# First layer of a convolution-attention network: the softmax denominators of two query blocks formed together on the rows of the taps

## The chip, the cores and the metric

The kernel runs on one core of a Trainium2 chip. The metric is device time in microseconds (us) of one execution; the median of three runs before the change is 6046.56 us (6038.23 to 6056.44). The core has a matrix engine (PE, with its weight loads PEld), a vector engine (DVE), a scalar engine (ACT), a general engine (POOL) and a queue for DMAs (SP), each with its own instruction stream in order. Matmul results land in PSUM, in eight banks of 128 partitions x 512 float32 each. All data here are float32.

## The reference, cut to what matters

Two images of 512 channels x 64 x 64 positions pass through four layers. The first layer, the only one that the change touches, is an attention with 8 heads of 64 channels. Each query looks at 9 local keys (a 3x3 window, the "taps") and at 256 pooled keys, with one softmax over both:

```python
attn_local = jnp.einsum('bhnd,bhndk->bhnk', q_scaled, k_local)
attn_pool = jnp.einsum('bhnd,bhpd->bhnp', q_scaled, _l2norm(k_pool))
attn = jax.nn.softmax(jnp.concatenate([attn_local, attn_pool], axis=-1), axis=-1)
a_local, a_pool = (attn[..., :ll], attn[..., ll:])
lt = jnp.einsum('bhnd,hdk->bhnk', q_norm, learnable_tokens) + learnable_bias[None] + a_local
x_local = jnp.einsum('bhnk,bhndk->bhnd', lt, v_local)
x_pool = jnp.einsum('bhnp,bhpd->bhnd', a_pool, v_pool)
```

So each query and head has one denominator, the sum of 9 + 256 exponentials, and its reciprocal is needed twice: on the 9 local weights, before a learned term is added, and on the 64 channels of the pooled part.

## The kernel before, in words

Class Local computes the first layer. A unit is 128 channels (two heads) and 1024 queries (two blocks j = 0, 1 of 512), so there are 16 units per image, and a loop in run() goes through them as a pipeline. One pass of the loop for unit u projects k, q and v of later units (projections, norms, value; L133 is the matmul of project), forms the tap products of unit u + 1 (tap_products, L1972, and tap_sums, L1985 and L2000), attends for unit u (attend) and weighs for unit u - 1 (weigh). The stages are generators that are advanced one step each per round, ten or so rounds per pass; this gives the order in which instructions are written down. It is a priority, not the final order: the program's builder moves an instruction ahead of an earlier one on the same engine when it finds the earlier one not ready, and then fixes the order.

What the prediction's steps touch:

- PSUM: five banks named mm are shared by all of these matmuls; one bank (tap) holds the tap sums and two (qs) a copy of the queries. A matmul that finds no free mm bank waits until ACT or DVE has read one out.
- attend, block by block: scores (L2017) and exponentials (L2021) for two halves of the 256 pooled keys; values (L2027), copied out by ACT (L2029); POOL adds the exponentials of the two halves (L2031). Then the denominators: two matmuls with ones over these sums (L2036) and two over el, the exponentials of the taps (L2040), give psD, in which the 64 rows of each head hold its denominator. DVE takes the reciprocal in two halves (L2049) and POOL multiplies the attended values by it (L2051). Block 0 does this in rounds 4 and 5, block 1 in rounds 7 and 8.
- el has four groups of 32 rows, two per block; of a group 18 rows are in use, 9 taps of head 0 and then 9 of head 1, and the even and odd taps lie in different groups. It is ready one pass before attend needs it.
- weigh, rounds 1 to 9 of the next pass: four matmuls (L2085) pick the reciprocals of the two heads and put them on the tap rows in PSUM; DVE multiplies el by them (L2087) and adds the learned part (L2088). Then for each tap and block a matmul spreads the weight to the channels (L2096), DVE multiplies it with the shifted values (L2102) and POOL adds the product to the attended values (L2107). Taps 6 and 7 fall in round 8, tap 8 in round 9. The result goes to DRAM.
- norms in round 1: four matmuls spread the norms of the new k and q (L1897), and DVE multiplies them in (L1905), which frees four mm banks. In round 8 POOL takes a power (L1932) for the next norms.
- output, in the last three passes and after: the output projection (L1808), with POOL additions of the bias (L1813) and DVE work (L1814, L1815).

Of the kernel before, what the change touches and what calls it, by code (L numbers as in the profile page):

```python
# [11 lines left out]
ALU = mybir.AluOpType  # L12
# [3 lines left out]
P = 128  # L16
C = 512
# [3 lines left out]
TB = 512  # L21
# [10 lines left out]
(C_ID, C_GRP, C_MEAN, C_ONE, C_E2, C_TAP, C_Y, C_X, C_MH, C_ROW, C_TAPW, C_E32, C_SR,  # L32
    C_SD) = (0, 128, 256, 384, 512, 514, 540, 572, 573, 589, 717, 757, 789, 821)
C_N = 949
# [1512 lines left out]
class Local:  # L1547
# [9 lines left out]
    def __init__(self, net, X, Y, sp_scale, d, wp, yp, pp, ppt, pps):  # L1557
# [18 lines left out]
        late = new([P, 12 * TB + 3 * TB], "late")  # L1576
# [4 lines left out]
        self.recips = part.ring([P, TB], 2)  # L1581
# [3 lines left out]
        self.gelus = Lent(late[:, 12 * TB:]).ring([P, TB], 3)  # L1585
# [391 lines left out]
    def tap_sums(self, u):  # L1977
# [4 lines left out]
        def sums(k):  # L1982
            for j in range(2):
                q = 2 * j + k % 2
                nc.tensor.matmul(ps[32 * q:32 * q + 32, :],  # L1985
                                 self.cst[:, C_TAPW + 8 - k:C_TAPW + 40 - k],
                                 self.prods[k % 3][:, j * TB:(j + 1) * TB], start=(k < 2),
                                 stop=(k > 6))
# [15 lines left out]
    def attend(self, u):  # L2004
# [5 lines left out]
        prob, R = {}, []  # L2010
        self.out[u] = out, R
# [11 lines left out]
        def values(j):  # L2023
# [5 lines left out]
            nc.scalar.copy(out[:, j * TB:(j + 1) * TB], psO)  # L2029
            for h in range(2):  # L2030
                nc.gpsimd.tensor_tensor(prob[j, 1][h], prob[j, 0][h], prob[j, 1][h], ALU.add)  # L2031

        def sums(j):
            psD = self.bank()
            for h, c in enumerate(heads):
                nc.tensor.matmul(psD[c, :], self.net.one[:, :HD], prob[j, 1][h], start=True,  # L2036
                                 stop=False)
            b = slice(j * HD, (j + 1) * HD)
            for h, c in enumerate(heads):
                nc.tensor.matmul(psD[c, :], self.cst[b, C_SD + h * HD:C_SD + (h + 1) * HD],  # L2040
                                 el[b, :], start=False, stop=True)
            return psD

        def ends(j, psD):
            r = self.recips()

            for i in range(2):
                part = slice(i * TB // 2, (i + 1) * TB // 2)
                nc.vector.reciprocal(r[:, part], psD[:, part])  # L2049
            o = out[:, j * TB:(j + 1) * TB]  # L2050
            nc.gpsimd.tensor_tensor(o, o, r, ALU.mult)  # L2051
            R.append(r)
# [9 lines left out]
        n = sums(0)  # L2062
        exponentials(1, 1)
        yield
        ends(0, n)
# [3 lines left out]
        n = sums(1)  # L2069
        yield  # L2070
        ends(1, n)
        yield

    def weigh(self, u):
# [3 lines left out]
        out, R = self.out.pop(u)  # L2078
        el, lt = self.el.pop(u), self.lt.pop(u)
        yield  # L2080
        ps = self.bank()
        for j in range(2):
            for g in range(2):
                q = 2 * j + g
                nc.tensor.matmul(ps[32 * q:32 * q + 32, :], self.cst[:, C_SR:C_SR + 32], R[j],  # L2085
                                 start=True, stop=True)
        nc.vector.tensor_tensor(el, el, ps, ALU.mult)  # L2087
        nc.vector.tensor_tensor(el, el, lt, ALU.add)  # L2088
        yield
# [75 lines left out]
def arrays_of(i):  # L2165
# [19 lines left out]
    cst[:HD, C_TAPW + 8] = 1  # L2185
# [3 lines left out]
    row = p % 32  # L2189
    cst[0, C_SR:C_SR + 9] = 1  # L2190
    cst[HD, C_SR + 9:C_SR + 18] = 1
    for h in range(2):
        mine = (row // 9 == h) & (row % 9 % 2 == p // 32 % 2)
        cst[:, C_SD + h * HD:C_SD + (h + 1) * HD] = mine[:, None]
# [22 lines left out]
    for q in range(4):  # L2217
        vec[32 * q:32 * q + 18, V_LBR:V_LBR + 4] = vec[:18, V_LB:V_LB + 4]
# [5 lines left out]
    tapb[:, :18] = taps  # L2224
# [7 lines left out]
        "taps": taps, "tapb": tapb.reshape(P, 9, P), "tok32": np.pad(tok, ((0, 0), (0, 0), (0, 14))),  # L2232
# [31 lines left out]
```

## Time and profile before

| what | value |
|---|---|
| median of 3 runs | 6046.56 us (6038.23 to 6056.44) |
| profiled execution | 6069.55 us, its span 6067.8 us |
| mean granted PE clock | 0.954 |
| PE busy in the span | 5607.9 us (92%) |
| DVE, ACT, POOL busy | 3101.9, 1466.3, 1604.9 us |
| first layer's units, first image, 300 to 1250 us | PE 913.24, DVE 540.37, POOL 589.59 us |
| first layer's units, second image, 3370 to 4290 us | PE 884.45, DVE 536.80, POOL 579.77 us |

In the group lines below, a line names the source line, the engine, the operation, the tiles written and read with their shapes, the count; then total busy time and mean ns of one; then the engine's idle time just before and what ended it. A matmul in float32 has two records. In the timeline lines, the columns are start and duration in us, engine, line, operation, tiles, and in brackets the idle time before and its releaser. A window line gives the window, its length, the busy time and count of PE, PEld, DVE, ACT and POOL, the granted PE clock, and the DMAs' share and GB/s.

### The profile page before, as it was taken

To read this page: it belongs to the slowest core of one execution; us is meant where nothing else is said; L and a number is where in the kernel's file an instruction comes from. 1 tells how busy PE (TensorE), PEld (TensorE's weight loads), DVE (VectorE), ACT (ScalarE), POOL (GpSimd) and SP (SyncE) were. 2 spreads that over 40 slices of the span, in tenths; PEclk is the share of its full clock that TensorE was granted. 3 is DMA by queue.
4 is the path that set the end of the run, shared out by engine and by line. 5 is a ranking of instruction groups with operands and counts; after the bars stand their busy time and mean duration, and the time that the engine had idled before them with its cause. 6 is when DMAs were issued, how large, how long until landed. Compare 5 with 4: busy or idle time off the path is not lost. (4 is left out here: it accounts for less than half of the span.)

```text
span 6067.8 us, 54683 instructions
## 1 busy us (share of the span) xinstructions
PE 5607.9 (92%) x21859; PEld 2361.9 (39%) x21859; DVE 3101.9 (51%) x3462; ACT 1466.3 (24%) x2633; POOL 1604.9 (26%) x1218
## 2 busy tenths in 40 slices
PE   7899999999978899999988999999999788999999
PEld 3333332455323344444343333324553334444443
DVE  3245556644669533444432555566456794334444
ACT  1232222114212222212112332220242132221221
POOL 0146657710320011100001566676003100110000
PEclk9899998999989999999988999999999899999999
DMA  3000000100000000100010000001000000000000
GB/s 131 2 6 16 13 12 30 47 35 9 1 0 0 29 1 1 56 14 35 28 51 2 6 16 16 11 28 52 30 9 0 0 0 16 1 8 9 20 14 22
DMA packets 50812, 118.32 MB, mean 20 GB/s; under 512 B 4018, under 2 KB 17074, under 8 KB 48756
## 3 DMA queue, kind: packets, MB, share of 16 engines
q1 hardware_dynamic: 50548, 114.73, 5.3%
q8 instruction: 175, 2.87, 0.2%
q14 instruction: 89, 0.73, 0.0%
HBM read 74.87 MB, written 39.85 MB: 19 GB/s over the span
## 5 line engine op out<-in xcount | busy, mean ns | idle before, releaser
L133 PE MATMUL mm<-big,w 128*128 128x512 f32 x2560 | 1219.1, 622 | 0.0
L2107 POOL TENSOR_TENSOR late<-late,big 128x512 f32<-128x512 f32 x576 | 717.3, 1277 | 523.3 <-DVE big L2102 511.5
L133 PEld LDWEIGHTS mm<-big,w 128*128 128x128 f32 x2560 | 479.4, 197 | 720.5 <-issue 623.9
L2102 DVE TENSOR_TENSOR big<-big,mm 128x512 f32<-128x512 f32 x576 | 363.2, 679 | 602.5 <-PE mm L2096 548.2
L1097 PE MATMUL acc<-big,dg 128*128 128x512 f32 x896 | 407.4, 614 | 79.8 <-DVE big L692 51.1
L692 DVE TENSOR_TENSOR big<-big 128x3968 f32<-128x3968 f32 x96 | 410.8, 4289 | 38.4 <-PE acc L1097 32.6
L1166 POOL TENSOR_TENSOR total<-prob 128x512 f32<-128x512 f32 x128 | 159.7, 1269 | 769.8 <-ACT prob L1163 769.8
L1430 DVE TENSOR_REDUCE tops<-mm 128x2 f32<-128x512 f32 x256 | 159.4, 681 | 290.8 <-PE mm L1271 290.8
L1242 POOL TENSOR_TENSOR sq<-q 128x512 f32<-128x512 f32 x64 | 66.6, 1041 | 905.6 <-ACT q L1240 905.6
L1097 PEld LDWEIGHTS acc<-big,dg 128*128 128x128 f32 x896 | 173.8, 197 | 312.0 <-issue 283.0
L1478 DVE RECIPROCAL recip<-psD 128x512 f32<-128x512 f32 x64 | 214.9, 3358 | 151.6 <-PE psD L1474 151.6
L2096 PE MATMUL mm<-late,tapb 18*128 18x512 f32 x1152 | 240.7, 665 | 54.0 <-DVE big L2102 28.3
L1183 DVE RECIPROCAL recip<-psD 128x512 f32<-128x512 f32 x64 | 214.9, 3358 | 87.1 <-PE psD L1180 87.1
L1330 ACT ACTIVATE big<-mm 128x512 f32<-128x512 f32 x256 | 153.1, 598 | 382.3 <-DVE top L1327 381.9
L1972 DVE TENSOR_TENSOR prod<-qs,big 128x1024 f32<-128x1024 f32 x192 | 228.9, 1207 | 29.3 <-PE tap L1985 29.3
L2049 DVE RECIPROCAL late<-mm 128x256 f32<-128x256 f32 x128 | 218.9, 1735 | 33.5 <-PE mm L2040 33.5
L133 PE MATMUL mm<-big,big 128*128 128x512 f32 x512 | 234.0, 619 | 0.0
L1309 PE MATMUL mm<-w,big 128*128 128x512 f32 x512 | 231.3, 601 | 0.0
L1932 POOL TENSOR_TENSOR wide<-norms,mhalf 128x32 f32<-128x32 f32 x34 | 185.1, 5443 | 168.6 <-DVE norms L1929 168.6
L133 PE MATMUL mm<-big,wq 128*128 128x512 f32 x512 | 228.7, 597 | 0.0
L547 PE MATMUL mm<-big,wo 128*128 128x512 f32 x512 | 224.5, 596 | 0.0
L547 PE MATMUL mm<-q,w 128*128 128x512 f32 x512 | 224.2, 596 | 0.0
(343 smaller groups left out, 7910.4 us busy)
## 6 DMA issues: line engine op xcount, KB each, us to landing
big<-in_x SPq DMA_DIRECT2D x8, 2048.0 KB, 10.6
yd<-late SPq DMA_DIRECT2D x32, 512.0 KB, 2.6
out<-big SPq DMA_DIRECT2D x16, 1024.0 KB, 4.2
big<-in_W_kv SPq DMA_DIRECT2D x8, 1024.0 KB, 11.1
big<-yd SPq DMA_DIRECT2D x16, 512.0 KB, 3.7
wd<-big SPq DMA_DIRECT2D x6, 1024.0 KB, 4.8
w<-wd SPq DMA_DIRECT2D x24, 256.0 KB, 3.0
prod<-yd SPq DMA_DIRECT2D x8, 512.0 KB, 4.3
```

The source lines that it names most:

```text
L133: self.nc.tensor.matmul(ps, w[:, kc, :], X[:, kc, blk * TB:(blk + 1) * TB], start=(kc == 0), stop=(kc == KC - 1))
L547: nc.tensor.matmul(ps, w[:, kc, oc * P:(oc + 1) * P], att[:, kc, :], start=(kc == 0), stop=(kc == KC - 1))
L692: nc.vector.tensor_tensor(o, a, b, ALU.max)
L1097: nc.tensor.matmul(accs[b], dg, src[:, b * TB:(b + 1) * TB], start=(j == 0), stop=(j == 6))
L1183: nc.vector.reciprocal(r, psD)
L1309: nc.tensor.matmul(ps, X[:, kc, lo:lo + P], wv[:, kc, :], start=(kc == 0), stop=(kc == KC - 1))
L1478: nc.vector.reciprocal(r, psD)
L1972: self.nc.vector.tensor_tensor(self.prods[k % 3].rearrange("p (y x) -> p y x", x=W), qs, self.kx[:, y + dy:y + dy + self.UY, dx:dx + W], A ...
L2049: nc.vector.reciprocal(r[:, part], psD[:, part])
L2096: nc.tensor.matmul(ps, self.tapb[32 * q:32 * q + 18, kk, :], el[32 * q:32 * q + 18, :], start=True, stop=True)
L2102: nc.vector.tensor_tensor(dst[:, j * TB:(j + 1) * TB].rearrange("p (y x) -> p y x", x=W), self.vx[:, y:y + self.UY // 2, dx:dx + W], ps.re ...
L2107: nc.gpsimd.tensor_tensor(o, o, dst[:, j * TB:(j + 1) * TB], ALU.add)
```

## The change

The tap rows of el are ordered tap by tap with the heads alternating (row 2 x tap + head) instead of head by head, and the constants follow. The sums of both blocks now go into one bank, once per unit: block j takes the 64 rows from 64 x j, and within them even rows hold head 0's denominator, odd rows head 1's (constants C_EVEN and C_SD). These rows line up with el's. So there is one reciprocal of 128 x 512 per unit (still in two halves), kept in a buffer of its own, and DVE multiplies el by it directly, from SBUF. For the channels, weigh spreads rows 64 x j and 64 x j + 1 of the reciprocal by one matmul per block with C_ROW, and DVE multiplies the attended values by the two banks; POOL's two multiplications are gone. The sums of the exponentials of block 0 go to buffers of their own (halves), since they are read later. The denominators are formed in rounds 7 and 8 for both blocks.

```diff
@@ -29,9 +29,9 @@
 RISKS = 16
 
 
-(C_ID, C_GRP, C_MEAN, C_ONE, C_E2, C_TAP, C_Y, C_X, C_MH, C_ROW, C_TAPW, C_E32, C_SR,
-    C_SD) = (0, 128, 256, 384, 512, 514, 540, 572, 573, 589, 717, 757, 789, 821)
-C_N = 949
+(C_ID, C_GRP, C_MEAN, C_ONE, C_E2, C_TAP, C_Y, C_X, C_MH, C_ROW, C_TAPW, C_E32, C_EVEN,
+    C_SD) = (0, 128, 256, 384, 512, 514, 540, 572, 573, 589, 717, 765, 797, 863)
+C_N = 927
 
 V_BQ, V_BK, V_BSR, V_LNG, V_LNB, V_QE, V_TEMP = 0, 4, 12, 16, 20, 24, 28
 V_WOFF, V_BOFF, V_BOUT, V_B2, V_B1, V_LB, V_WOFF2 = 32, 33, 34, 38, 42, 43, 47
@@ -1573,16 +1573,18 @@
         self.weighed = [weighed[:, i * self.UT:(i + 1) * self.UT] for i in range(2)]
         self.prods = [whole.take([P, self.UT])] + [new([P, self.UT], f"prod{i}") for i in range(2)]
         self.tok = whole.take([P, KC, 32])
-        late = new([P, 12 * TB + 3 * TB], "late")
+        late = new([P, 13 * TB + 3 * TB], "late")
         part = Lent(late)
         self.prob = part.ring([P, TB], 4)
         self.att = part.ring([P, self.UT], 2)
         self.els = part.ring([P, TB], 2)
-        self.recips = part.ring([P, TB], 2)
+
+        self.halves = [part.take([P, TB]) for _ in range(2)]
+        self.recip = part.take([P, TB])
         self.lts = part.ring([P, TB], 3)
 
         self.first = Lent(late[:, :12 * TB])
-        self.gelus = Lent(late[:, 12 * TB:]).ring([P, TB], 3)
+        self.gelus = Lent(late[:, 13 * TB:]).ring([P, TB], 3)
         self.raw_w = [w.rearrange("p (kc o) -> p kc o", kc=KC)
                       for w in (weighed, flat[:, 6144:8192])]
         self.w_sr = qs[:, :KC * C].rearrange("p (kc o) -> p kc o", kc=KC)
@@ -1983,7 +1985,7 @@
             for j in range(2):
                 q = 2 * j + k % 2
                 nc.tensor.matmul(ps[32 * q:32 * q + 32, :],
-                                 self.cst[:, C_TAPW + 8 - k:C_TAPW + 40 - k],
+                                 self.cst[:, C_TAPW + 16 - 2 * k:C_TAPW + 48 - 2 * k],
                                  self.prods[k % 3][:, j * TB:(j + 1) * TB], start=(k < 2),
                                  stop=(k > 6))
 
@@ -2007,8 +2009,8 @@
         cc = u // self.UN
         qs, el = self.qs[u % 3], self.el[u]
         out = self.att()
-        prob, R = {}, []
-        self.out[u] = out, R
+        prob = {}
+        self.out[u] = out
         heads = [slice(h * HD, (h + 1) * HD) for h in range(2)]
 
         def exponentials(j, k2):
@@ -2027,65 +2029,60 @@
                     nc.tensor.matmul(psO[c, :], self.vp[:, k2, cc * P + h * HD:][:, :HD],
                                      prob[j, k2][h], start=(k2 == 0), stop=(k2 == 1))
             nc.scalar.copy(out[:, j * TB:(j + 1) * TB], psO)
+            dst = prob[1, 1] if j else self.halves
             for h in range(2):
-                nc.gpsimd.tensor_tensor(prob[j, 1][h], prob[j, 0][h], prob[j, 1][h], ALU.add)
-
-        def sums(j):
+                nc.gpsimd.tensor_tensor(dst[h], prob[j, 0][h], prob[j, 1][h], ALU.add)
+
+        def sums():
             psD = self.bank()
-            for h, c in enumerate(heads):
-                nc.tensor.matmul(psD[c, :], self.net.one[:, :HD], prob[j, 1][h], start=True,
-                                 stop=False)
-            b = slice(j * HD, (j + 1) * HD)
-            for h, c in enumerate(heads):
-                nc.tensor.matmul(psD[c, :], self.cst[b, C_SD + h * HD:C_SD + (h + 1) * HD],
-                                 el[b, :], start=False, stop=True)
+            blocks = [slice(j * HD, (j + 1) * HD) for j in range(2)]
+            for h in range(2):
+                for j, b in enumerate(blocks):
+                    nc.tensor.matmul(psD[b, :], self.cst[:, C_EVEN + h:C_EVEN + h + HD],
+                                     (prob[1, 1] if j else self.halves)[h], start=(h == 0),
+                                     stop=False)
+            for b in blocks:
+                nc.tensor.matmul(psD[b, :], self.cst[b, C_SD:C_SD + HD], el[b, :], start=False,
+                                 stop=True)
             return psD
 
-        def ends(j, psD):
-            r = self.recips()
-
-            for i in range(2):
-                part = slice(i * TB // 2, (i + 1) * TB // 2)
-                nc.vector.reciprocal(r[:, part], psD[:, part])
+        exponentials(0, 0)
+        yield
+        exponentials(0, 1)
+        yield
+        values(0)
+        yield
+        exponentials(1, 0)
+        yield
+        exponentials(1, 1)
+        yield
+        values(1)
+        yield
+        yield
+        psD = sums()
+        yield
+
+        for i in range(2):
+            part = slice(i * TB // 2, (i + 1) * TB // 2)
+            nc.vector.reciprocal(self.recip[:, part], psD[:, part])
+        yield
+
+    def weigh(self, u):
+
+        nc = self.nc
+        cc, y0 = u // self.UN, u % self.UN * self.UY
+        out, R = self.out.pop(u), self.recip
+        el, lt = self.el.pop(u), self.lt.pop(u)
+        yield
+        banks = [self.bank() for _ in range(2)]
+        for j, ps in enumerate(banks):
+            q = slice(64 * j, 64 * j + 2)
+            nc.tensor.matmul(ps, self.cst[q, C_ROW:C_ROW + P], R[q, :], start=True, stop=True)
+        nc.vector.tensor_tensor(el, el, R, ALU.mult)
+        nc.vector.tensor_tensor(el, el, lt, ALU.add)
+        for j, ps in enumerate(banks):
             o = out[:, j * TB:(j + 1) * TB]
-            nc.gpsimd.tensor_tensor(o, o, r, ALU.mult)
-            R.append(r)
-
-        exponentials(0, 0)
-        yield
-        exponentials(0, 1)
-        yield
-        values(0)
-        yield
-        exponentials(1, 0)
-        yield
-        n = sums(0)
-        exponentials(1, 1)
-        yield
-        ends(0, n)
-        values(1)
-        yield
-        yield
-        n = sums(1)
-        yield
-        ends(1, n)
-        yield
-
-    def weigh(self, u):
-
-        nc = self.nc
-        cc, y0 = u // self.UN, u % self.UN * self.UY
-        out, R = self.out.pop(u)
-        el, lt = self.el.pop(u), self.lt.pop(u)
-        yield
-        ps = self.bank()
-        for j in range(2):
-            for g in range(2):
-                q = 2 * j + g
-                nc.tensor.matmul(ps[32 * q:32 * q + 32, :], self.cst[:, C_SR:C_SR + 32], R[j],
-                                 start=True, stop=True)
-        nc.vector.tensor_tensor(el, el, ps, ALU.mult)
-        nc.vector.tensor_tensor(el, el, lt, ALU.add)
+            nc.vector.tensor_tensor(o, o, ps, ALU.mult)
         yield
         for k in range(0, 9, 2):
             banks = {}
@@ -2182,16 +2179,14 @@
 
     cst[:, C_ROW:C_ROW + P] = p[:, None] % 32 == p[None, :] // HD
 
-    cst[:HD, C_TAPW + 8] = 1
+    cst[:HD, C_TAPW + 16] = 1
     cst[HD:, C_TAPW + 17] = 1
     cst[:, C_E32:C_E32 + 2] = p[:, None] // HD == np.arange(2)
 
-    row = p % 32
-    cst[0, C_SR:C_SR + 9] = 1
-    cst[HD, C_SR + 9:C_SR + 18] = 1
-    for h in range(2):
-        mine = (row // 9 == h) & (row % 9 % 2 == p // 32 % 2)
-        cst[:, C_SD + h * HD:C_SD + (h + 1) * HD] = mine[:, None]
+    row, half = p % 32, np.arange(HD)
+    cst[:, C_EVEN:C_EVEN + 66] = np.arange(66) % 2 == 0
+    mine = (row < 18) & (row // 2 % 2 == p // 32 % 2)
+    cst[:, C_SD:C_SD + HD] = mine[:, None] & (row[:, None] % 2 == half % 2)
     g = np.stack(np.meshgrid(np.arange(16), np.arange(16), indexing="ij")).reshape(1, 2, NK)
     a = {k: np.asarray(v) for k, v in i.items()}
 
@@ -2215,13 +2210,14 @@
     vec[:18, V_LB:V_LB + 4] = a["L0_conv_learnable_bias"].reshape(KC, 18).T
     vec[:, V_LBR:V_LBR + 4] = 0
     for q in range(4):
-        vec[32 * q:32 * q + 18, V_LBR:V_LBR + 4] = vec[:18, V_LB:V_LB + 4]
+        for h in range(2):
+            vec[32 * q + h:32 * q + 18:2, V_LBR:V_LBR + 4] = vec[9 * h:9 * h + 9, V_LB:V_LB + 4]
     vec[:, V_WOFF2:V_WOFF2 + 2] = np.tile(a["L1_conv_w_off2"].T, (2, 1))
 
     taps = (np.arange(18)[:, None, None]
             == 9 * (p[None, None, :] // HD) + np.arange(9)[None, :, None]).astype(f)
     tapb = np.zeros((4, 32, 9, P), f)
-    tapb[:, :18] = taps
+    tapb[:, :18] = taps.reshape(2, 9, 9, P).transpose(1, 0, 2, 3).reshape(18, 9, P)
     tok = np.zeros((P, KC, 18), f)
     t = a["L0_conv_learnable_tokens"].reshape(KC, 2, HD, 9).transpose(1, 2, 0, 3)
     tok[:HD, :, :9] = t[0]
@@ -2229,9 +2225,12 @@
     arrays = {
         "x": a["x"], "cst": cst, "grid": np.broadcast_to(g, (P, 2, NK)).astype(f),
         "vec": vec, "tok": tok,
-        "taps": taps, "tapb": tapb.reshape(P, 9, P), "tok32": np.pad(tok, ((0, 0), (0, 0), (0, 14))),
-
-        "row2": (p[:, None] % 32 == 2 + p[None, :] // HD).astype(f), "bv_row": b_kv[None, C:], "pb_rows": np.broadcast_to(a["L0_conv_b_proj"], (P, C)),
+        "taps": taps, "tapb": tapb.reshape(P, 9, P),
+        "tok32": np.pad(tok.reshape(P, KC, 2, 9).transpose(0, 1, 3, 2).reshape(P, KC, 18),
+                        ((0, 0), (0, 0), (0, 14))),
+
+        "row2": (p[:, None] % 32 == 2 + p[None, :] // HD).astype(f), "bv_row": b_kv[None, C:],
+        "pb_rows": np.broadcast_to(a["L0_conv_b_proj"], (P, C)),
         "bproj_row": a["L0_conv_b_proj"][None, :],
         "W_q": a["L0_conv_W_q"], "W_kv": a["L0_conv_W_kv"], "W_sr": a["L0_conv_W_sr"],
         "W_proj": a["L0_conv_W_proj"],
```

## The prediction

> **What bounds the kernel now.** I read the page first (span 6067.8 us, run 6069.55 us, median of the runs 6046.56 us), then windows by stage, the groups of the lines that the diff touches, one period engine by engine, and the waits.
>
> Busy time by window, second image, two periods (us; PE, PEld, DVE, ACT, POOL):
>
> ```profile
> 3799.30:3854.00 54.70, 53.36 (x210) 16.92 (x212) 31.88 (x40) 16.61 (x27) 35.20 (x26) 1.00 0.04 15
> 3854.00:3908.70 54.70, 53.36 (x210) 16.91 (x212) 31.88 (x40) 16.62 (x27) 35.20 (x26) 1.00 0.03 10
> ```
>
> A unit costs 54.70 us and PE is busy for 53.36 of them. There are 16 units per image and two images, so 1 us per unit is 32 us. PE works in order, so a late bank or operand stops all behind it. DVE (31.9) and POOL (35.2) have slack on average, not everywhere.
>
> Groups that the diff touches (busy, mean ns):
>
> ```profile
> L2049 DVE RECIPROCAL late<-mm 128x256 f32<-128x256 f32 x128 | 218.9, 1735 | 33.5 <-PE mm L2040 33.5
> L2051 POOL TENSOR_TENSOR late<-late 128x512 f32<-128x512 f32 x64 | 81.9, 1279 | 52.9 <-DVE late L2049 28.6 <-issue 15.1 <-ACT late L2021 6.5
> L2087 DVE TENSOR_TENSOR late<-late,mm 128x512 f32<-128x512 f32 x32 | 21.7, 677 | 0.4 <-PE mm L2085 0.4
> L2088 DVE TENSOR_TENSOR late<-late 128x512 f32<-128x512 f32 x32 | 56.3, 1758 | 1.0
> ```
>
> L2087 and L2088 have one shape, yet L2088 averages 1758 ns: its median is 692, its longest 9371. The timeline of DVE shows where:
>
> ```profile
> 3997.56 0.68 DVE L2087 TENSOR_TENSOR late<-late,mm 128x512 f32<-128x512 f32 x1
> 3998.27 9.37 DVE L2088 TENSOR_TENSOR late<-late 128x512 f32<-128x512 f32 x1
> ```
>
> and that of POOL over the same time:
>
> ```profile
> 3994.79 2.51 POOL L2107 TENSOR_TENSOR late<-late,big 128x512 f32<-128x512 f32 x2
> 3997.26 9.84 POOL L1813 TENSOR_TENSOR big<-big,kp 128x512 f32<-128x512 f32 x8
> ```
>
> L2088 adds two SBUF operands. It could not finish until eight back-to-back POOL additions were through; it did not slip in between two of them. L2087, L2102 and L1972 have one operand in PSUM and keep 0.68 and 1.2 us beside a busy POOL.
>
> The stretch where this matters, DVE in one period:
>
> ```profile
> 3822.75 1.75 DVE L2049 RECIPROCAL late<-mm 128x256 f32<-128x256 f32 x1
> 3825.84 0.69 DVE L2102 TENSOR_TENSOR big<-big,mm 128x512 f32<-128x512 f32 x1 [1.34 <-POOL late L2107]
> 3827.06 0.69 DVE L2102 TENSOR_TENSOR big<-big,mm 128x512 f32<-128x512 f32 x1 [0.54 <-POOL late L2107]
> 3827.67 1.22 DVE L1972 TENSOR_TENSOR big<-qs,big 128x1024 f32<-128x1024 f32 x1
> 3828.80 2.35 DVE L1972 TENSOR_TENSOR prod<-qs,big 128x1024 f32<-128x1024 f32 x2
> 3831.07 1.27 DVE L1905 TENSOR_TENSOR big<-big,mm 128x512 f32<-128x512 f32 x2
> 3833.45 0.68 DVE L2087 TENSOR_TENSOR late<-late,mm 128x512 f32<-128x512 f32 x1
> ```
>
> and POOL:
>
> ```profile
> 3824.52 4.98 POOL L2107 TENSOR_TENSOR late<-late,big 128x512 f32<-128x512 f32 x4
> 3829.43 1.30 POOL L2051 TENSOR_TENSOR late<-late 128x512 f32<-128x512 f32 x1
> 3830.65 2.55 POOL L2107 TENSOR_TENSOR late<-late,big 128x512 f32<-128x512 f32 x2
> ```
>
> POOL is busy without a gap from 3824.52 to 3833.20, and L2087 starts just after. And PE hangs on L1905 there (weight loads):
>
> ```profile
> 3831.80 0.29 PEld L2017 LDWEIGHTS mm<-big,kp 64*128 64x128 f32 x2 [0.92 <-DVE big L1905]
> 3833.45 0.30 PEld L133 LDWEIGHTS mm<-big,w 128*128 128x128 f32 x2 [0.76 <-DVE qn L1905]
> ```
>
> L1905 frees the banks for the next scores and the value projection: DVE has no slack here.
>
> [...] all PSUM readers in the page are DVE or ACT. [...] four 128x32 matmuls of L2085 took 1.0 us in all, as much as two 128x64 of L2036.
>
> **The change part by part**, per unit, from starts in this period.
> 1. First block's sums, gone: L2036 and L2040, 1.01 us each: -2.02 on PE. A 0.38 us bank wait before L2036 passes to the next scores.
> 2. The joint sums: four 128x64 (L2027 has this shape: 1.87 a call) and a pair of 64x64 (1.01) make 2.88 instead of 2.02. They end at 3816.01 + 2.88 = 3818.9, where the reciprocal began at 3818.76, and PE waits there anyway (L1985 at 3819.10, next matmul at 3821.11, of which 1.0 is work). So +0.2 of the +0.86 is on the path; without that wait all is.
> 3. Two reciprocal halves fewer, -3.37 on DVE, at 3853.98: worth 0, since DVE idles 7.71 us soon after. The other two halves stay.
> 4. L2051 twice, -2.56 on POOL: nothing waits for the first; the second shortens POOL's run to 3831.9.
> 5. The spread: two 2x128 matmuls for four 128x32: two row groups of L2096 took 1.06 us against 1.0, so 0. But it takes two of five banks, freed only after L1905 and the two new products on DVE: the second must await an L1905 that the scores awaited before. One L1905 step, 0.6; I take +0.5.
> 6. The two products of the attended values on DVE: no row has exactly this; L2102 has one SBUF and one PSUM operand, 0.68 each. They fall into the 4.45 us that DVE idles after 3834.86: 0; with that cover gone, 1.36.
> 7. el times R: as L2087, but R now lies in SBUF. Alone it costs 0.69, as L2088. Its place is the question.
>
> **Where el times R goes.** The order on an engine isn't that of the source: a second reciprocal half runs after four L2102, and two L1972 of later priority run ahead of L1905, which was not ready. L2087 ran late because it needed PE's spread. The new product needs only R and el, both done by 3824.5. By priority it comes after the L1972 of round 0 and ahead of the next two and, until PE delivers, of L1905. So it reaches DVE's head at 3828.8, in POOL's run. It waits to 3831.9 and ends at 3832.6; one L1972 (1.13) follows, and perhaps el+lt (0.62) and another L1972 (1.13), and L1905 starts at 3833.7 to 3835.5 instead of 3831.07: 2.7 to 4.4 late, I take 3.5. PE is late by as much.
> Sum: -2.02 + 0.2 + 0.5 + 3.5 = +2.2 per unit (1.4 to 3.1). Eleven weighing periods per image have both POOL's run behind them and L1905: 22 x 2.2 = +48 (31 to 68).
> Twice per image L1813 follows the run at once, so the product waits for both: to 4007.1 - 1.3 = 4005.8. L1905 then starts near 4008.5 and PE's L2096 near 4016, against 4007.79: about 8 late, less 1.8: +6.3, four times +25 (22 to 29). The first and the last two weighings per image meet an almost quiet POOL: 6 x -1.3 = -8.
> Total +65 (45 to 89): 6069.6 to 6135 for the profiled run, 6046.6 to **6112** for the median, 6070 to 6160 with the spread of the runs (18 us). The granted clock (0.94 to 1.00 by window) may give some back when PE idles.
>
> **Rivals.**
> - *Faster*: el times R runs behind L1905, at 3833.45 as L2087 did, after POOL's run. Then a unit gains 2.02 - 0.2 - 0.5 = 1.3: 32 x 1.3 = -42, 6005 (5990 to 6028). For it: DVE is in order and L2087 stands there now. Against: only its need of PE put it there. It decides if L1905 is delayed by under 1.3 us.
> - *Even*: the product is early but L1905 runs right after it, and PE has other work ready, so the delay is near 1.3: 6047, within 18. Against: the earliest end is already 3832.6.
> - *Slower still*: the product comes right after the reciprocal, at 3824.5, ahead of both L2102. It waits for POOL to run dry at 3829.5; both L2102 (1.3) and one to three more follow. L1905 is 3.8 to 5 late: 22 x 3.1 + 25 - 8 = +85, 6132 (6115 to 6150). Against: L2102 has the earlier round and now runs first.
>
> **How the numbers follow.** Forecast 0.57, slower still 0.13, faster 0.18, even 0.12. A measurement can tell 0.3% (18 us). Slower gets 0.57 + 0.13, and a little of the even case; same about 0.11; faster 0.18. The forecast's own range is 6070 to 6160. Leaving out most of the faster case (0.12) and the top (0.06), the range is 6012 to 6160.
>
> **What would show it.** Right: a two-SBUF DVE product at its new line averaging 2 to 5 us instead of 0.69, ended with a POOL L2107 group; PE weight loads waiting on L1905 for 3 us and more per period; periods of 56 to 58 us at full clock. Part 1 right: L1985 of round 4 about 2 us earlier after the second score pair. Wrong: if that product runs in 0.69 us each time, the periods should be near 53.4 us and the total near 6005. Also wrong if POOL lets DVE in between two additions, or if PE fills the wait with other matmuls.

## The result and the profile after

The changed kernel takes 6080.28 us (median of 4 runs, 6074.2 to 6085.03) against 6042.4 us (4 runs, 6036.85 to 6056.44): a ratio of 1.0059, 95% interval 1.0038 to 1.0080. It is slower by 38 us, where 65 were forecast. The span of its profiled execution is 6081.4 us against 6067.8 before, 13.6 us more. The two differences disagree since the profiled execution of the kernel before was itself 27 us over its median.

A period in a window of the changed kernel, second image, in the columns of the windows before (granted PE clock third from the end), and then stretches of that period, cut at PE's wait:

```profile
3835.80:3893.80 58.00, 55.33 (x204) 17.93 (x206) 30.46 (x38) 16.69 (x28) 33.66 (x24) 0.94 0.02 9
3845.80:3847.80 2.00, 2.00 (x12) 0.89 (x10) 2.00 (x2) 1.08 (x2) 2.00 (x2) 1.00 0.00 0
3847.80:3850.30 2.50, 0.50 (x3) 0.00 (x0) 2.50 (x5) 0.00 (x0) 1.88 (x2) 0.76 0.00 0
3850.30:3852.30 2.00, 1.96 (x2) 0.49 (x2) 2.00 (x4) 0.19 (x1) 0.00 (x0) 0.50 0.65 262
3852.30:3854.30 2.00, 2.00 (x5) 0.50 (x4) 0.97 (x2) 1.05 (x1) 0.00 (x0) 0.50 0.00 0
3854.30:3858.70 4.40, 4.40 (x10) 1.79 (x8) 0.00 (x0) 1.09 (x2) 2.48 (x2) 0.81 0.00 0
```

A period has gone from 54.70 to 58.00 us. DVE and POOL have less to do (31.88 to 30.46, 35.20 to 33.66). PE had 2.02 us taken off and 0.86 put on, so its busy time should have fallen by 1.16; it rose, from 53.36 to 55.33. The cut shows why: within the 2.5 us in which PE works for 0.50, its clock goes to half. By the clock records it is at half from 3849.11 to 3855.93, so it falls while PE still waits. So of the 3.3 us, -1.16 is the work, +1.33 is idle time (2.67 against 1.34), and some +3.1 is the same work at a lower clock. (Part of this stretching falls where PE would have waited; an experiment below puts the clock's net part at 2.5.)

The groups that the diff touches:

```profile
L2067 DVE RECIPROCAL late<-mm 128x256 f32<-128x256 f32 x64 | 111.4, 1749 | 21.3 <-PE mm L2045 21.3
L2081 DVE TENSOR_TENSOR late<-late 128x512 f32<-128x512 f32 x32 | 43.8, 1368 | 0.0
L2082 DVE TENSOR_TENSOR late<-late 128x512 f32<-128x512 f32 x32 | 27.6, 861 | 0.1
L2085 DVE TENSOR_TENSOR late<-late,mm 128x512 f32<-128x512 f32 x64 | 40.9, 674 | 0.0
```

L2081 is el times R, L2082 adds the learned part; the latter averaged 1758 ns before. Line numbers have moved: L1905 is now L1907, L1972 is L1974, L1985 is L1987, L2017 is L2019, L2107 is L2104. DVE in one period of the changed kernel, from its timeline:

```profile
3843.84 0.69 DVE L2099 TENSOR_TENSOR big<-big,mm 128x512 f32<-128x512 f32 x1 [0.54 <-POOL late L2104]
3844.44 1.22 DVE L1974 TENSOR_TENSOR big<-qs,big 128x1024 f32<-128x1024 f32 x1
3845.57 1.25 DVE L2081 TENSOR_TENSOR late<-late 128x512 f32<-128x512 f32 x1
3846.74 1.21 DVE L1974 TENSOR_TENSOR prod<-qs,big 128x1024 f32<-128x1024 f32 x1
3847.88 0.67 DVE L2082 TENSOR_TENSOR late<-late 128x512 f32<-128x512 f32 x1
3848.48 1.21 DVE L1974 TENSOR_TENSOR prod<-qs,big 128x1024 f32<-128x1024 f32 x1
3849.61 1.27 DVE L1907 TENSOR_TENSOR big<-big,mm 128x512 f32<-128x512 f32 x2
```

POOL's run beside it, six additions in one line of its timeline:

```profile
3841.32 8.36 POOL L2104 TENSOR_TENSOR late<-late,big 128x512 f32<-128x512 f32 x6
```

The place is as forecast: el times R runs right after the first L1974, within POOL's run of six additions, and el plus lt one L1974 later. But L2081 takes 1.25 us and not 3.8. L1907 starts 5.17 us after the first L1974; before, L1905 did so after 3.40 wherever it didn't have to wait for PE itself (six of the ten inner periods of the second image; 3.95 to 5.66 us in the others). PE's weight loads in that stretch, with the loader's idle time in brackets:

```profile
3847.17 0.29 PEld L2080 LDWEIGHTS mm<-late,cst 2*128 2x128 f32 x2 [0.20 <-ACT late L2023]
3850.34 0.49 PEld L2080 LDWEIGHTS mm<-late,cst 2*128 2x128 f32 x2 [2.87 <-DVE big L1907]
3852.34 0.50 PEld L2019 LDWEIGHTS mm<-big,kp 64*128 64x128 f32 x4 [1.50 <-DVE qn L1907]
3854.34 0.50 PEld L133 LDWEIGHTS mm<-big,w 128*128 128x128 f32 x2 [1.50 <-issue]
```

The weight load of the spread's second matmul comes after 2.87 us without a load, held up by a bank from L1907. Part of that time the matmuls before it still run; the matmul line has what PE itself loses, 2.04 us:

```profile
3850.34 2.07 PE L2080 MATMUL mm<-late,cst 2*128 2x512 f32 x2 [2.04 <-DVE big L1907]
```

The 0.49 and 0.50 us of the loads after it, where the same loads took 0.30 before, are the half clock again.

### The profile page after: what moved, and what is told of

The parts are those of the page before. It is cut to its first block, busy times and chain, and to the rows that moved or that the text cites. A ratio compares the mean times of both kernels' runs of the same rounds, so it can differ in the third digit from the quotient of the medians.

```text
span 6081.4 us, 53921 instructions
## 1 busy us (share of the span) xinstructions
PE 5614.1 (92%) x21603; PEld 2385.9 (39%) x21603; DVE 3030.8 (50%) x3462; ACT 1468.7 (24%) x2633; POOL 1551.1 (26%) x1154
## 5 line engine op out<-in xcount | busy, mean ns | idle before, releaser
L133 PE MATMUL mm<-big,w 128*128 128x512 f32 x2560 | 1212.0, 618 | 0.0
L2104 POOL TENSOR_TENSOR late<-late,big 128x512 f32<-128x512 f32 x576 | 740.4, 1318 | 484.7 <-DVE big L2099 484.5
L133 PEld LDWEIGHTS mm<-big,w 128*128 128x128 f32 x2560 | 477.4, 196 | 719.2 <-issue 627.9
L2099 DVE TENSOR_TENSOR big<-big,mm 128x512 f32<-128x512 f32 x576 | 362.9, 680 | 688.5 <-PE mm L2093 642.0
L1974 DVE TENSOR_TENSOR prod<-qs,big 128x1024 f32<-128x1024 f32 x192 | 232.8, 1216 | 57.5 <-PE tap L1987 57.5
L2093 PE MATMUL mm<-late,tapb 18*128 18x512 f32 x1152 | 237.1, 648 | 19.1 <-DVE big L2099 13.5
L133 PE MATMUL mm<-big,big 128*128 128x512 f32 x512 | 234.2, 619 | 0.0
L2034 POOL TENSOR_TENSOR late<-late 128x512 f32<-128x512 f32 x128 | 160.2, 1273 | 273.1 <-ACT late L2023 159.8
L133 PE MATMUL mm<-big,wq 128*128 128x512 f32 x512 | 229.3, 599 | 0.0
```

Source lines behind the costliest of these rows:

```text
L133: self.nc.tensor.matmul(ps, w[:, kc, :], X[:, kc, blk * TB:(blk + 1) * TB], start=(kc == 0), stop=(kc == KC - 1))
L1974: self.nc.vector.tensor_tensor(self.prods[k % 3].rearrange("p (y x) -> p y x", x=W), qs, self.kx[:, y + dy:y + dy + self.UY, dx:dx + W], A ...
L2093: nc.tensor.matmul(ps, self.tapb[32 * q:32 * q + 18, kk, :], el[32 * q:32 * q + 18, :], start=True, stop=True)
L2099: nc.vector.tensor_tensor(dst[:, j * TB:(j + 1) * TB].rearrange("p (y x) -> p y x", x=W), self.vx[:, y:y + self.UY // 2, dx:dx + W], ps.re ...
L2104: nc.gpsimd.tensor_tensor(o, o, dst[:, j * TB:(j + 1) * TB], ALU.add)
```

## The experiments

The clock records of the trace give when PE ran at half. The table is from the traces: ten inner periods of the second image (from the first unit's result going out to the eleventh's), how much of them was at half clock, and the start of L1907 (or its like) after the first L1974 in most of them (for the kernel before in six of ten, see above). The ratio is that of the medians to the kernel before on the same chip.

| kernel | median us | ratio (95%) | ten periods, us | at half clock | L1907 after L1974 |
|---|---|---|---|---|---|
| before | 6042.4 | 1 | 558.2 (first image 568.1) | 27.3 (52.3) | 3.40 |
| after | 6080.28 | 1.0059 (1.0038 to 1.0080) | 581.0 | 68.9 | 5.17 |
| e1_el_on_pool | 6037.89 | 0.9968 (0.9955 to 0.9980) | 559.9 | 47.9 | 3.40 |
| e2_spread_later | 6123.22 | 1.0094 (1.0064 to 1.0124) | 597.4 | 85.3 | 5.16 |
| e3_pool_and_later | 6067.17 | 1.0015 (1.0000 to 1.0031) | 573.7 | 61.7 | 3.40 |
| e4_filler | 6084.47 | 1.0046 (1.0035 to 1.0057) | 576.0 | 47.2 | 5.16 |
| e5_phase | 6086.62 | 1.0047 (1.0029 to 1.0065) | 580.9 | 68.9 | 4.83 |
| e6_tap_bank | 6017.80 | 0.9943 (0.9924 to 0.9962) | 549.7 | 37.7 | 3.40 |
| e7_before_two_ops | 6107.49 | 1.0086 (1.0057 to 1.0115) | 579.2 | 50.9 | 5.10 |
| e8_fill_five | 6090.19 | 1.0078 (1.0051 to 1.0105) | 579.1 | 3.4 | |
| e9_fill_early | 6097.20 | 1.0088 (1.0070 to 1.0107) | 588.3 | 8.6 | |
| e10_fill_three | 6076.46 | 1.0042 (1.0027 to 1.0056) | 573.7 | 27.3 | |

Three causes stood beside each other at the start: the two instructions on DVE ahead of L1907, the second bank of the spread, and the clock.

**e1: el's two instructions on POOL.**

```diff
-        nc.vector.tensor_tensor(el, el, R, ALU.mult)
-        nc.vector.tensor_tensor(el, el, lt, ALU.add)
+        nc.gpsimd.tensor_tensor(el, el, R, ALU.mult)
+        nc.gpsimd.tensor_tensor(el, el, lt, ALU.add)
```

> The changed kernel with el times R and el plus lt on POOL instead of DVE; nothing else. DVE-order theory (these two instructions stand ahead of L1907 on DVE, 1.77 us with the wait for POOL, and so start PE's idle time): L1907 starts 3.4 us after the round's first L1974 as in the kernel before, PE waits about 0.7 us for the second spread bank instead of 2.5, its clock stays full, a period is 53.5 to 54.5 us instead of 58.0 and the total near 5990. Bank theory (the second bank of the spread is the cause whatever DVE does): PE still waits about 2 us there, periods stay above 57, total within 20 us of 6080.

It is faster than both kernels: 0.9968 of the time before. L1907 is back at 3.40 us. PE's second spread matmul and its loads in a period of the second image:

```profile
3684.77 1.12 PE L2080 MATMUL mm<-late,cst 2*128 2x512 f32 x2 [0.27 <-DVE big L1907]
3684.77 0.29 PEld L2080 LDWEIGHTS mm<-late,cst 2*128 2x128 f32 x2 [1.10 <-DVE big L1907]
3685.82 0.64 PEld L2019 LDWEIGHTS mm<-big,kp 64*128 64x128 f32 x4 [0.76 <-DVE big L1907]
3687.95 0.50 PEld L133 LDWEIGHTS mm<-big,w 128*128 128x128 f32 x2 [1.50 <-DVE late L2085]
```

The loader's gap before L1907's bank is 1.10 us instead of 2.87, and PE's own idle time 0.27 instead of 2.04: 1.77 less each time, which is what L1907 is earlier, so the two instructions on DVE account for the difference. What is left is a small bank wait, and half clock (0.50 us loads again): it falls in every period, for 3.4 or 6.8 us, with 0.27 us of idle time before it. The total misses the forecast of 5990 and the periods, 55.4 and 56.9 us, are above it; the forecast had the clock full.

**e2 and e3: the spread and its products one round later**, with el on DVE (e2) and on POOL (e3). The edit of e2; e3 has gpsimd in its two el lines:

```diff
         el, lt = self.el.pop(u), self.lt.pop(u)
         yield
+        nc.vector.tensor_tensor(el, el, R, ALU.mult)
+        nc.vector.tensor_tensor(el, el, lt, ALU.add)
+        yield
         banks = [self.bank() for _ in range(2)]
         for j, ps in enumerate(banks):
             q = slice(64 * j, 64 * j + 2)
             nc.tensor.matmul(ps, self.cst[q, C_ROW:C_ROW + P], R[q, :], start=True, stop=True)
-        nc.vector.tensor_tensor(el, el, R, ALU.mult)
-        nc.vector.tensor_tensor(el, el, lt, ALU.add)
         for j, ps in enumerate(banks):
             o = out[:, j * TB:(j + 1) * TB]
             nc.vector.tensor_tensor(o, o, ps, ALU.mult)
-        yield
```

> The changed kernel with the spread to the channels and its two products one round later, just before the first tap products; el's two instructions stay ahead of L1907 on DVE. Bank theory: PE no longer waits for a spread bank in round 1, the idle time goes, period 54 to 55 us, total near 6000. DVE-order theory: the next scores need a bank that L1907 frees, as the spread did, so PE idles about as long (2 us or more), the clock still drops, period 57 to 58 us, total 6060 to 6085.

> Both edits together: el's two instructions on POOL, spread and products one round later. Both theories: no wait over 1 us on PE in round 1, clock full, period 53 to 54 us, total 5975 to 6000. If the two causes add, it is faster than either alone by 0.5 us per period (15 us); if one suffices, it equals that one within 10 us.

Both totals are above all that was forecast. With el on DVE (e2) the wait only changes its owner, from the second matmul of the spread to the second pair of scores, in PE's loads of e2:

```profile
3588.88 0.50 PEld L2019 LDWEIGHTS mm<-big,kp 64*128 64x128 f32 x2 [2.28 <-DVE big L1907]
```

The time rises to 1.0094 with more half clock than anywhere else. So taking the spread's banks out of this round doesn't remove the wait: L1907's lateness is the cause, and whoever needs a bank next pays.

With el on POOL as well (e3), no matmul waits for L1907 any more, and yet it is 29 us worse than e1, on the same chip. Its clock falls in another place, here at 3847.86, in windows of e3:

```profile
3841.03:3847.86 6.83, 6.83 (x29) 2.14 (x29) 2.65 (x5) 1.38 (x2) 2.44 (x3) 1.00 0.08 32
3847.86:3851.27 3.41, 3.41 (x14) 0.45 (x10) 1.03 (x2) 0.59 (x1) 3.41 (x4) 0.50 0.00 0
```

By the profile PE was busy without a gap for the 6.83 us before. In the last 3.4 of them it ran matmuls of few rows or columns: the spread of both blocks (L2083, 2 rows), the spread of tap weights (L2093, 18 rows) and the start of L2029 (64 columns). So here, with PE busy for 6.83 of 6.83 us, no idle time was needed for the clock to fall to 0.50. How much of the 29 us is the clock isn't separated.

**e7: the two instructions put into the kernel before**, with nothing else of the change (their result goes to a spare buffer).

```diff
+        self.spare = new([P, 480], "spare")
...
+        nc.vector.tensor_tensor(self.spare, el[:, :480], R[1][:, :480], ALU.mult)
+        nc.vector.tensor_tensor(self.spare, self.spare, lt[:, :480], ALU.add)
```

> The kernel before, with nothing of the change, plus two VectorE products of SBUF by SBUF (128x480, their result goes to a spare buffer that nothing reads) between the tap sums of round 0 ahead of L1905, where the change puts el times R and el plus lt. Theory 'two instructions ahead of L1905 are the cost': L1905 starts 1.5 to 2.5 us later, TensorE waits that much longer for its banks, periods go from 54.7 to 57.5 to 58 to 61, total 50 to 90 us over the kernel before. Rival 'the cost comes from the spread's two banks or the joint sums': the total is within 20 us of the kernel before.

The total is 52 us over the kernel before, within the forecast of 50 to 90, and most periods take 56.4 to 59.7 us, a little under the forecast. L1906 (L1905 of before) starts 5.10 us after the first tap sum, 1.70 later. This kernel keeps full clock through some periods, so it gives the price apart from the clock. One of them as a window:

```profile
3576.00:3632.30 56.30, 53.29 (x210) 16.88 (x208) 33.49 (x41) 16.60 (x27) 36.02 (x25) 1.00 0.04 14
```

Such periods take 56.4 us from result to result, 1.7 more than the 54.7 of before, with PE's busy time unchanged (53.29 against 53.36). A delay of L1905 by 1.70 costs 1.7 us: DVE has no slack there, as the prediction said. It also confirms that the order of DVE's instructions alone brings such a loss, without the joint sums or the spread.

**e5: does the moment of el times R's arrival decide how long it waits?** Arrivals in the kernel before with 0.27 and 0.42 us left of a POOL addition had waited 9.37 and 8.30 us, those with 0.69 and more had got in after that one addition. A small instruction ahead of the first L1974 moves the arrival:

```diff
+            part = el[:, :TB // 2].rearrange("p (n o) -> p n o", o=1)
+            nc.vector.tensor_reduce(el[:, :TB // 2], part, AX.X, ALU.add)
```

> The changed kernel with one small VectorE instruction more (about 0.37 us: it copies the first 256 columns of el onto themselves), in round 0 ahead of the tap sums, so that el times R reaches GpSimd's addition about 0.3 us later than in the changed kernel, with some 0.35 us of it left instead of 0.69. Theory 'the phase of the arrival decides': el times R then waits through the additions that follow till GpSimd's run is dry, 3 us or more instead of 1.24; L1907 starts about 7.5 us after the first tap sum instead of 5.2; periods of 60 us and more; total 6120 to 6150. Rival 'it always gets in after the addition under way': el times R takes 0.95 to 1.0 us, L1907 starts about 5.3 us after the first tap sum, periods near 58.0, total 6080 to 6095.

The rival's numbers came: 0.91 us, periods of 58.0, 6086.62 us. DVE's timeline of e5:

```profile
3849.20 0.91 DVE L2083 TENSOR_TENSOR late<-late 128x512 f32<-128x512 f32 x1
```

It arrived with 0.36 to 0.38 us left in 24 of 32 units and got in after that addition each time. Yet over the traces of after, e2, e4 and e7, the eight arrivals with 0.33 or 0.34 us left all waited through two to five additions more (3.3 to 7.0 us), and all that came with 0.5 to 1.2 us left got in after the addition under way or found POOL's run ended. Two arrivals of e5 at the change from one addition to the next waited through the new one and another (3.0 us). In all of these long waits the product ended 0.52 to 0.55 us after the last addition before POOL's next pause. So there are two outcomes: it gets in after one addition, or it waits until POOL's run is over. This isn't drawn at random, since within each kernel the same timing gave the same outcome; but the time left doesn't decide it alone: 0.42 waits and 0.36 doesn't. What else enters stays open. With 0.36 to 0.38 us left the experiment lay between arrivals that waited (0.33, 0.34 and 0.42), so it could not find it.

**e4, e8, e10 and e9: PE kept busy while it waits.** Extra matmuls of 128x512 into the taps' bank, which is free then, between the two matmuls of the spread: two (e4), five (e8), three (e10); e9 has two ahead of the first matmul and three behind it. e4's edit; the others change the count or the place:

```diff
-        ps = self.ppt.tile([P, TB], F32, name="tap")
+        ps = self.tap_ps = self.ppt.tile([P, TB], F32, name="tap")
...
             nc.tensor.matmul(ps, self.cst[q, C_ROW:C_ROW + P], R[q, :], start=True, stop=True)
+            if j == 0 and u < KC * self.UN - 2:
+                for _ in range(2):
+                    nc.tensor.matmul(self.tap_ps, self.net.ident, self.X[:, 0, :TB], start=True,
+                                     stop=True)
```

> The changed kernel with two idle-time matmuls of 128x512 (0.93 us each at full clock, into the tap bank before it is begun, result overwritten) between the two spread matmuls of each unit: extra work of 1.9 us per period, and the outputs are unchanged. Clock theory (PE idles 2.5 us, its clock then falls to half for 6.8 us, and most of the 58.0 us comes from that): the filler keeps the clock up at no cost, since it lies in the wait; period 55 to 56 us, total 6010 to 6035. Without the clock's part (the wait alone costs the time): period 58.0 or longer, total 6080 or more.

> The changed kernel with five extra 128x512 matmuls into the taps' bank between the two matmuls of the spread (e4_filler had two), in all units but the last two; outputs unchanged. They fill nearly all of TensorE's 2.87 us wait for the second bank. Theory 'TensorE's idling takes the clock down': no half-clock stretch is left in the inner periods, each of them takes 55.5 to 56.2 us, total 6015 to 6040. Rival 'the small matmuls ahead of the wait (one-row and two-row ones, L1892 to the spread) take it down, the idling only follows': half-clock stretches stay in most periods, as in e4_filler, periods of 58 to 60 us, total 6080 to 6120.

> The same five extra matmuls, but two of them ahead of the first matmul of the spread and three behind it, so that the stretch of small matmuls is broken up too. If TensorE's idling alone takes the clock down, as e8_fill_five: 6015 to 6040 for both. If the small matmuls do it, this kernel has fewer half-clock stretches than e8_fill_five and is faster by 20 us or more.

> The changed kernel with three extra matmuls between the two of the spread: each is two passes of 0.45 us, so the three take 2.7 us, about the 2.87 us that TensorE waits there (two, 1.8 us, left half-clock stretches in about half the periods; five, 4.5 us, left nearly none but cost 1.6 us more than the wait). Theory 'the idling takes the clock down, and the change without that is about even': half-clock stretches in at most 3 of the 10 inner periods of an image, the others 55.5 to 56.2 us, total 6010 to 6050, below the changed kernel's 6080. Rival 'three are still too few': stretches in half the periods or more, 58 us and over, total 6070 to 6095.

The clock theory's totals were missed in all four; those of e4, e8 and e10 came where the rivals had put them, and e9 fits neither forecast. An extra matmul has two passes of 0.45 us, so five take 4.5 us where PE idles 2.04, which the forecast of e8 had overlooked: from totals alone the clock theory would be rejected. The clock records answer. With five, 3.4 us of ten periods are at half clock instead of 68.9, and a period of e8 in a window is at full clock throughout:

```profile
3629.20:3686.90 57.70, 57.08 (x212) 19.02 (x210) 30.54 (x39) 16.72 (x27) 33.67 (x23) 1.00 0.03 10
```

The small matmuls ahead of the wait are all still there, so here they alone don't bring the clock down, and with the idle stretch filled by matmuls of all 128 rows it stays up. In e3 it fell, to 0.50, with small matmuls and no idle time before it (6.83 us). e9, which breaks up the small ones too, is no better (8.6 us at half clock), and slower: 58.5 us a period against 57.7. With two fillers the periods vary (55.5, 56.8, 58.4 and 60.1 us). With three, eight of ten periods still have some 3 us at half clock, where the changed kernel has 6.8. So the filler's length, or where it falls, matters, and the exact condition isn't settled.

One line of e4 is worth more than its total. Its fillers fit into the wait (two take 1.8 of the 2.04 us), so its periods at full clock show the changed kernel without the clock's part:

```profile
3666.90:3722.40 55.50, 54.76 (x206) 18.02 (x204) 30.48 (x39) 16.61 (x27) 33.69 (x24) 1.00 0.03 10
```

That is 55.5 us against 54.7 before, also at full clock, and 58.0 after: at most 0.8 us of the 3.3 is the change's own balance of waits and gains, and some 2.5 is the clock, if the fillers gain nothing by themselves.

**e6: e1 with the first block's spread in the taps' bank**, so that the spread needs one of the shared banks, as before.

```diff
-        ps = self.ppt.tile([P, TB], F32, name="tap")
+        ps = self.tap_ps = self.ppt.tile([P, TB], F32, name="tap")
...
-        banks = [self.bank() for _ in range(2)]
+        shared = u < KC * self.UN - 2
+        banks = [self.tap_ps if shared else self.bank(), self.bank()]
```

> e1_el_on_pool, with the first block's spread written to the taps' bank of PSUM, which is free from el's exponential to round 2 (in all units but the last two, which keep the two banks of before). The two spreads then need only one bank that L1907 frees, as in the kernel before. Theory 'the second bank's wait is what is left of the cost': TensorE's 1.10 us wait ahead of the second spread and the 1.50 us ahead of the norms' product both go, 0.5 to 2 us less per period than e1_el_on_pool, total 6000 to 6030 against its 6038. Rival 'the clock takes it': half-clock stretches stay in each period and the total is within 10 us of e1_el_on_pool.

6017.8 us, 0.9943 of the time before: the fastest of all, some 20 us under e1 (the ratios are from two chips, and their intervals overlap by a little). The spread no longer waits, but the scores do, in PE's loads of e6:

```profile
3848.08 0.29 PEld L2081 LDWEIGHTS mm<-late,cst 2*128 2x128 f32 x2
3849.47 0.29 PEld L2019 LDWEIGHTS mm<-big,kp 64*128 64x128 f32 x2 [1.10 <-DVE big L1907]
3851.12 0.30 PEld L133 LDWEIGHTS mm<-big,w 128*128 128x128 f32 x2 [0.76 <-DVE qn L1907]
```

The sentence of the forecast that these waits would be gone was wrong: the 1.10 us (again 0.27 us of idle time on PE) has gone one step down the line and not away; what goes is one step of the queue behind it. The ten periods are 10 us shorter than e1's, and 10 us of half clock less are among them, so how much is the bank and how much the clock isn't separated.

## Why the prediction came out as it did

The direction was right, for the reason given: the two products ahead of L1907 on DVE make PE wait. 6080 lies in the range, but that the sum came near is in part luck, since errors of both signs cancel. By its steps:

- **1, first block's sums.** Right in kind. In round 4 from L2096 to L1985, the stretch took 1.52 + 2.02 + 1.06 = 4.60 us before; now 1.43 + 1.60 = 3.03. So 1.57 of the 2.02 us is kept: the bank wait passed on to the scores, as written, but larger.
- **2, joint sums.** Right: 2.87 us instead of 2.02, and L1987 behind them takes 1.41 instead of 2.01, so +0.25 net where +0.2 stood.
- **3 and 4, reciprocals and POOL's products.** DVE and POOL each have about 1.5 us less per period, and no period is shorter for it. Nothing here measured the two apart.
- **5, the spread's second bank.** The place was right: it is the instruction that waits for L1907. Its +0.5 was not measured alone; e6 with its 1.0 us per period bounds it, the clock included.
- **6, two products on DVE.** Hidden in the changed kernel: L133's load, 1.50 us after the one before it, waits for nothing of DVE's. In e1, where L1907 is early, it is L2085 that releases this load, but PE shows no idle time there either.
- **7, el times R.** This is the step that failed in size. The order on DVE was forecast instruction by instruction. But the wait for POOL was taken as lasting till POOL's run ends (3.1 us), from the 9.37 us of one L2088. It is 0.55 us in 24 of 32 units: "POOL lets DVE in between two additions", which the text had listed as what would make it wrong. So el times R costs 1.17 us net and el plus lt 0.60: L1907 is 1.77 later, not 3.5. That the wait lasts so long was half right: the long waits of the experiments do last till POOL's run ends, but arrivals in the inner periods get in earlier. The prediction's criterion, a product averaging 2 to 5 us, was not met (1.37). Nor was PE's wait of 3 us and more: its loads wait 2.87, its matmuls 2.04. The prediction read "waits" off the loads, where even before, 0.92 us stood with no idle time on PE.
- **The clock.** The text said that it may give some back when PE idles. The sign was wrong. With the new wait the clock goes to half for 6.8 us in every period, 2.5 us of loss, more than what L1907's delay nets; e8 shows that it isn't so where the wait is filled (3.4 us in ten periods). The periods of 56 to 58 us that the prediction named are there, but not "at full clock". In the clock records the stretches at 0.50 in the inner periods are 3.41, 6.83 or 10.24 us long (at 3541.65, 3483.62 and 1005.55 us of the kernel before). By an estimate from the 0.50 alone, which takes half of such a stretch as lost, 68.9 us in ten periods cost 3.4 each, where e4 shows 2.5. The prediction had read these windows' clocks (0.94 to 1.00) and not asked when they fall.
- **The last periods with L1813.** Forecast 25 us more in four periods, 8 less in six others. The last five periods of an image took 265.2 us before and 253.4 now (second image). Since el plus lt passes before POOL reaches L1813 (now L1815), the waits of 9.37 and 8.30 us are gone. DVE's timeline of the changed kernel there:

```profile
4070.51 1.23 DVE L2081 TENSOR_TENSOR late<-late 128x512 f32<-128x512 f32 x1
4072.80 0.68 DVE L2082 TENSOR_TENSOR late<-late 128x512 f32<-128x512 f32 x1
```

and POOL's timeline beside them, where L1815 starts after both:

```profile
4066.23 8.38 POOL L2104 TENSOR_TENSOR late<-late,big 128x512 f32<-128x512 f32 x6
4074.56 4.95 POOL L1815 TENSOR_TENSOR big<-big,kp 128x512 f32<-128x512 f32 x4
```

Together, by the profiled executions: the ten inner periods are 12.8 us longer in the first image and 22.8 in the second, the last five 12 shorter in each; with 2.6 us between the images this is the +13.6, to within a microsecond. The other 24 us of the +38 can't be placed, since there is no trace of an execution of the kernel before near its median. Had the kernel before kept full clock in all twenty inner periods (an estimate: 20 times 54.7, 1094 us), the change would have cost 68 us there; its own half-clock stretches, 52.3 us in the first image and 27.3 in the second, hid a part. Its executions range from 6039 to 6097 us in one set of 48, and the clock goes with it: the twelve shortest have a mean granted clock of 0.958 to 0.960, the eight longest one of 0.950 to 0.954. That the clock makes this spread is likely, but was not tested.

Of the rivals, "even" was nearest in the balance: at full clock the delay of L1907 (1.77) and the gains (1.57, less 0.25 for the joint sums) leave little. It set the break at 1.3 us, which is about right. But the order that it assumed, L1907 right behind the product, isn't what ran, and it lacked the clock.

## What to carry over

Price an instruction that is put ahead of another on an engine by who waits behind the second one: here 1.7 us on DVE cost 1.7 us of PE in each period (e7, 56.4 us against 54.7), though DVE idles two fifths of the time (busy for 31.88 of 54.70 us before), and the same two instructions on POOL did not delay that one at all. When PE is the bound, ask of each new wait not only how long it is but whether the clock falls with it; here 2.04 us of waiting came with 6.8 us at half clock, which cost some 2.5 us more. Where an instruction of one engine ends late beside another engine's work, look at several such instructions and at what was under way when each arrived: here one L2088 took 9.37 us, and L2081 1.25 us in most units.

## What the runs showed of the hardware

- Half-clock stretches and the loop's period went together. In the changed kernel the stretches of 6.8 us come every 58.0 us, 17 times the 3.413 us that the shortest of its half-clock records last, and the periods settle there in both images alike: 58.4, 58.2, 58.1, 58.1, 58.1 and then 58.0. Nearly the same in e5. In e8, with next to no half clock (3.4 us in ten periods), they are 57.7, no multiple of it. In the traces of the two kernels all half-clock records (63 before, 65 after) start whole multiples of 3.4133 us apart, to within 0.01 us, also where the period doesn't settle; it is the settling that speaks for a period locked by the clock. That it is locked is read from these numbers, and was not tested.
- Idle time on PE alone doesn't tell whether the clock falls. In the changed kernel it fell after 3.41 us with PE busy for 2.60, in e1 after 3.41 us with PE busy for 3.14, and in e3 after 6.83 us with PE busy throughout. What these stretches have in common is matmuls of few rows or columns; that these take the clock down is a reading, and was not tested apart. In the kernel before, 3.41 us with PE busy for 2.47 ended in a fall once (at 3483.62) and not another time (at 3596.26), so the busy time of such a stretch doesn't decide it alone; what does, no run here tells.
- DVE products with both operands in SBUF could end late beside POOL's additions. In the changed kernel L2081 waited for the addition under way alone (1.24 us in all, 24 of 32 units); over the traces of before, after, e2, e4, e5 and e7 such products did that or were passed by additions that followed until POOL paused, one to seven more (3.0 to 9.37 us). Where L2081 did get in, POOL's next addition took 1.72 us instead of 1.27. L2099, with one operand in PSUM, took at most 0.69 us, also beside a busy POOL.
